# Layer 0 of a four-layer graph network: one pair's term sums shared between ScalarE and VectorE, with a third PSUM double bank and more closely spaced row loads

## The chip, the cores and the metric

The kernel runs on one core of one Trainium2 chip. The metric is the device time of one execution in microseconds (us), as a median over runs. The engines are called PE (TensorE), DVE (VectorE), ACT (ScalarE), POOL (GpSimd) and SP (SyncE); PE accumulates into PSUM, 8 banks of 128 x 512 float32, and everything else lies in SBUF. SP and POOL issue most DMA transfers here.

## The reference

`x` has shape (8, 2048, 64): 8 batches, N = 2048 nodes, 64 channels. `adj` is a row-normalised 2048 x 2048 matrix. Four layers follow each other, each as `x = layernorm(x + layer(x))`:

```
layer 0:  x0 = x, x1 = A x, x2 = 2 A (A x) - x                    (K = 3 diffusion steps)
          w[n,k] = sum_d emb[n,d] * weight[d,k]   (d = 0..15),  b = emb @ bias
          out[n] = sum_k xk[n] @ w[n,k] + b[n]
layer 1:  e = leaky_relu(s1[i] + s2[j]), masked by adj > 0.5, softmax over j, att @ x, elu
layer 2:  (A + I) (x W^T + b) / degree
layer 3:  three steps of  v = relu([v, A v] W1^T + b1) W2^T + b2
```

In layer 0 the weight matrix differs from node to node, but only through the 16 numbers `emb[n, :]`. So the kernel multiplies every node's stacked vector by all 16 base matrices, which gives 16 results ("terms") of 64 channels each, and then sums the terms with the factors `emb[n, d]`.

## The kernel before

All work is float32 except the masks (bfloat16). The 8 batches form four pairs (`NPAIR = 4`); a pair's values `SX[p]` are 128 columns wide and 16 tiles of 128 nodes long. A product with the adjacency matrix is a "sweep" (`sweep`, line 1040): for each of four column chunks, a PSUM bank from `acc_ring` collects 16 matmuls of 128 x 512 (line 1059), whose moving operand comes in "a-tiles" of 512 KB that SP loads (`fetch`, line 223) into 7 buffers. The sweeps run in a fixed order: A x for pairs 0 and 1 together, then A(A x) for each pair with A x of pairs 2 and 3 mixed in, then for each pair one sweep of layer 2 and three of layer 3.

What runs between the matmuls of the sweeps is not written out by hand. Every piece of work is a generator that yields an engine and what it waits for; `Plan.go` (line 82) repeatedly picks the one that can begin first by the plan's own costs, with a rank as tie-break, and so writes one fixed instruction order for each engine. `Ring` (line 96) hands out buffers and remembers when each was planned to be free. At run time each engine follows its order and waits on semaphores, so a planned cost that is off shows as a wait.

`rows_of_adj` (line 400) loads the 16 row tiles of `adj` (1 MB each, on SP, into `bc_ring`, 4 buffers) at the due times in its `yield`. `row_tile` (line 411) sums each row on ACT (line 414) and makes the mask on DVE (lines 417 to 420), which POOL stores to DRAM (line 423). The row maxima of layer 1 (line 706) load these masks again.

`second_pass` (line 553) is the last part of layer 0. For each tile of 128 nodes it has two halves `h` of eight terms. A half is four 512-wide products (line 578) into a double bank `yp` from `pp_ring`, which has two of them. `add_terms` (line 590) then reads `yp`. If a "terms" buffer was free in `e_ring` (4 buffers, shared with layer 1's `e`), ACT scales each term by its factor into that buffer (line 599), for both halves, and DVE adds the 16 terms as a tree of widths 1024, 512 and 256 (line 612) and two adds into `SX[p]` (line 614). If none was free, DVE does all 16 terms by multiply-and-add straight from PSUM (line 601). `first_norm` (line 621) adds the bias (line 625) and normalises a chunk of four tiles.

When a pair's four chunks are normalised, `layer1` (line 635) transposes the values (line 647), computes the score vectors (line 657), turns them into rows (`to_rows`, line 754; matmul at 759) and broadcasts these by DMA (line 682). DVE then finds row maxima (line 706, 32 per pair), and `weights` (line 773) makes each attention tile on DVE (784, 797) and ACT (792, 800), which PE applies to the values (`po`, line 810). `po_ring` has one double bank. `finish` (line 828) ends a half of layer 1, from the matmuls `pf` (line 845) on. `layer2_tail` (line 943) multiplies by W (`ps_emb`, line 947) and adds on DVE (line 956); `start_chunk` (line 967) normalises (last step at line 487), transposes (`ps_vT`, line 981), and `u_chunk` (line 990) prepares the operand of the next sweep (`ps_u`, line 994), copied by `copy` (line 337).

PSUM's eight banks are: `acc` 2 single banks, `pp` 2 double banks, `po` 1 double bank.

Of the kernel before, what the change touches and what calls it, by code (L numbers as in the profile page):

```python
# [17 lines left out]
P = 128  # L18
# [3 lines left out]
CW = N // NCH  # L22
# [113 lines left out]
def resnorm_d4_kernel(  # L136
# [22 lines left out]
    plan = Plan()  # L159
    at = plan.at  # L160
# [15 lines left out]
    pp_ring = Ring(ps, "pp", 2)  # L176
    po_ring = Ring(ps, "po", 1)
    bc_ring = Ring(wp, "bc", 4)
# [18 lines left out]
    def batches(v):  # L197

        if len(v.shape) == 3:
            v = v.rearrange("p t n -> p (t n)")  # L200
        return v.rearrange("p (b c) -> p b c", c=C)
# [198 lines left out]
    def rows_of_adj():  # L400


        for t in range(NT):
            yield "SP", [115.0 + 13.0 * t, bc_ring]
            an, k = bc_ring.take([P, 2, HALF], "an")
            an = an.rearrange("p a b -> p (a b)")
            nc.sync.dma_start(an, adj[t * P : (t + 1) * P, :])
            done = plan.run("SP", 2.8, bc_ring.t, 115.0 + 13.0 * t) + 9.0
            plan.start(1, row_tile(t, an, k, done))

    def row_tile(t, an, k, done):
        yield "ACT", [done]
        dg = tiny([P, 1], "dg", 2)
        nc.scalar.activation(an, an, AF.Copy, accum_out=dg)
        done = plan.run("ACT", act(N) + 0.2, done)
        yield "DVE", [done, mr_ring]
        nc.vector.tensor_scalar_add(dg, dg, 1.0)
        nc.vector.reciprocal(rdeg[:, t : t + 1], dg)
        mk, km = mr_ring.take([P, N], "mr", BF16)
        nc.vector.tensor_scalar(mk, an, THRESHOLD, NEG_INF, ALU.is_le, ALU.mult)  # L420
        done = plan.run("DVE", 1.13 + 0.16, done)
        bc_ring.give(k, done)
        nc.gpsimd.dma_start(by_row[t], mk)
        done = plan.run("DMA", 0.6, done) + 4.0
        mr_ring.give(km, done)
        at["by_row", t] = done + 2.0
        if all(("by_row", i) in at for i in range(NT)):
            at["rows"] = done
# [124 lines left out]
    def second_pass():  # L553

        for n in range(NPAIR * NCH):
            yield "PE", [("y2", n + 1), ("xg", n + 1)]
            p, c, y2T, ky, got = queue[n]
            xg, kx = stacked[n]
            left = [TPC]
            for j in range(TPC):  # L560
                t = c * TPC + j
                cs = slice(j * P, (j + 1) * P)
                for h in range(2):
                    hs = slice(h * CW, (h + 1) * CW)
                    if h == 0 or pp_ring.ready() > plan.free["PE"]:
                        yield "PE", [("xg", n + 1), got, pp_ring]
                    if h == 0:


                        terms = None  # L570
                        if e_ring.ready() < NEVER:
                            terms = e_ring.take([P, D0, P], "terms")
                    yp, k = pp_ring.take([P, 2, CW], "yp")

                    for k2 in (h, 1 - h):
                        for e in range(2):
                            rows = slice(e * C, (e + 1) * C) if k2 else slice(0, P)
                            nc.tensor.matmul(  # L578
                                yp[:, e, :],
                                lhsT=y2T[rows, cs] if k2 else xg[:, e, cs],  # L580
                                rhs=(wk2 if k2 else w01)[rows, hs],
                                start=(k2 == h),
                                stop=(k2 != h),
                            )
                    t_pe = plan.run("PE", 2.8, got)
                    plan.start((2, 2, 1, 1)[p], add_terms(p, c, t, h, yp, k, terms, t_pe, left))
            yt_ring.give(ky, t_pe)
            xg_ring.give(kx, t_pe)

    def add_terms(p, c, t, h, yp, k, terms, t_pe, left):  # L590
        eng = "ACT" if terms else "DVE"
        yield eng, [t_pe]
        v = SX[p][:, t, :]
        for d in range(8):
            dd = h * 8 + d
            term = yp[:, :, d * C : (d + 1) * C]
            weight = emb_sb[:, t, dd : dd + 1]
            if terms:
                nc.scalar.activation(batches(terms[0][:, dd, :]), term, AF.Copy, scale=weight)  # L599
            else:  # L600
                nc.vector.scalar_tensor_tensor(
                    batches(v), term, weight, batches(v), ALU.mult, ALU.add
                )
        done = plan.run(eng, 8 * (0.25 if eng == "ACT" else 0.265), t_pe)
        pp_ring.give(k, done)
        if h == 0:
            return
        if terms:
            yield "DVE", [done]
            for half in (8, 4, 2):  # L610
                a, b = (terms[0][:, i * half : (i + 1) * half, :] for i in range(2))
                nc.vector.tensor_tensor(a, a, b, ALU.add)  # L612
            for d in range(2):
                nc.vector.tensor_tensor(v, v, terms[0][:, d, :], ALU.add)
            done = plan.run("DVE", 2.5, done)
            e_ring.give(terms[1], done)
        left[0] -= 1
        if left[0] == 0:
            plan.start(2, first_norm(p, c, plan.free["DVE"] + plan.LAG))

    def first_norm(p, c, done):
        yield "DVE", [done]
        v = SX[p][:, tiles(c), :]
        v4 = v.rearrange("p t (e c) -> p t e c", c=C)
        nc.vector.tensor_tensor(
            v4, v4, eb[:, tiles(c), :].unsqueeze(2).to_broadcast([P, TPC, 2, C]), ALU.add
        )
        done = plan.run("DVE", dve(CW), done)
        done = yield from layer_norm(v, CW, done)
        at["n0", p, c] = done  # L630
        if all(("n0", p, i) in at for i in range(NCH)):
            at["x1", p] = max(at["n0", p, i] for i in range(NCH))
# [494 lines left out]
    ctx.enter_context(tc.manual_schedule())  # L1127
    plan.start(0, constants())
    plan.start(1, rows_of_adj())
    plan.start(1, stacks())  # L1130
    plan.start(2, second_pass())
    plan.start(3, tails())
    for p in range(NPAIR):
# [41 lines left out]
```

## Time and profile before

| what | value |
|---|---|
| median of 3 runs | 2182.61 us (2180.09 to 2184.45) |
| profiled execution | 2179.89 us, of which the span from first to last instruction 2178.1 us |
| DVE, tree of adds (L612), 58 of each width | 1024 wide 1222 ns, 512 wide 692 ns, 256 wide 425 ns |
| ACT, terms (L599), 928 instructions | 251.8 us busy |
| DVE, multiply-and-add from PSUM (L601), 96 instructions | 33.7 us busy, mean 351 ns |
| DVE, row maxima (L706), 128 instructions | 292.8 us busy, mean 2287 ns; first at 377.5 us |
| SP, loads of adjacency rows (L407), 16 of 1 MB | issued from 116.4 to 316.5 us, median 8.7 us from issue to landing |

The profile page gives the busy time and share of each engine, and then the span in 40 equal slices, one digit each in tenths of busy time. A line of the waits view says which instruction group waited for which, for how many us in total, how often, and the longest one. A line of the timeline gives start, duration, engine, source line, the tiles written and read, and in brackets the idle time before it with what ended it. One PE matmul of 128 x 512 in float32 appears as two records; consecutive records overlap, so a mean duration of one (about 0.6 us) is longer than the distance from one to the next (0.43 us). The line numbers are those of the kernel before; in the kernel after, lines 590 to 611 lie up to 6 lower in the file and all later ones 7 lower.

### The profile page before, as it was taken

The numbers are of one execution on the slowest core, as the hardware profiler recorded it, in microseconds if no ns is written. First come the engines' busy times: TensorE is split into PE (matmuls) and PEld (weight loads), VectorE is DVE, ScalarE is ACT, GpSimd is POOL, SyncE is SP. The second block draws the span as 40 slices with busy tenths as digits, with TensorE's granted clock in tenths as the row PEclk, the third lists the DMA queues.
The fourth block names the chain that finished last, engine by engine and source line by source line (L and its number), as shares of the span: only waits on it lengthen the run. The fifth ranks groups of instructions, "written<-read, shape, count | busy, mean of one in ns | idle before, by whom it ended". The sixth has DMA issues, their size and how long they took to land. (4 is left out here: it accounts for less than half of the span.)

```text
span 2178.1 us, 19094 instructions
## 1 busy us (share of the span) xinstructions
PE 2116.7 (97%) x6421; PEld 934.0 (43%) x6421; DVE 1424.8 (65%) x1823; ACT 973.0 (45%) x1761; POOL 194.6 (9%) x342
## 2 busy tenths in 40 slices
PE   8999999999999999999999999999999999999997
PEld 3444444433443333335443444444444544444443
DVE  2215554999789999989998989989797400121002
ACT  0016664467776555675724757417476200111001
POOL 2210000110011010000001011011010000000000
PEclk9999999999999999999999999999999999999999
DMA  9798764564344473347689778788787777887785
GB/s 312 270 323 297 241 201 146 165 208 123 113 159 122 132 245 110 121 129 258 214 304 345 237 274 297 255 307 292 241 270 226 247 263 269 282 289 247 265 277 182
DMA packets 228453, 504.26 MB, mean 232 GB/s; under 512 B 20530, under 2 KB 28850, under 8 KB 224242
## 3 DMA queue, kind: packets, MB, share of 16 engines
q1 hardware_dynamic: 189378, 372.79, 51.0%
q0 software_dynamic: 34752, 128.14, 17.4%
q10 hardware_dynamic: 4224, 2.10, 0.4%
q8 instruction: 51, 0.84, 0.2%
q14 instruction: 48, 0.39, 0.1%
HBM read 471.31 MB, written 29.56 MB: 230 GB/s over the span
## 5 line engine op out<-in xcount | busy, mean ns | idle before, releaser
L1059 PE MATMUL acc<-a,SX 128*128 128x512 f32 x1536 | 693.8, 597 | 9.4 <-DMA SX<-in_x 6.4
L1059 PE MATMUL acc<-a,SA 128*128 128x512 f32 x1280 | 575.0, 596 | 8.9 <-ACT SA L337 4.8
L1059 PEld LDWEIGHTS acc<-a,SX 128*128 128x128 f32 x1536 | 285.6, 191 | 350.7 <-issue 336.4
L1059 PEld LDWEIGHTS acc<-a,SA 128*128 128x128 f32 x1280 | 238.8, 191 | 293.9 <-issue 278.6
L792 ACT ACTIVATE e<-e,sv 128x1024 f32<-128x1024 f32 x256 | 280.9, 1153 | 108.8 <-DVE e L784 107.3
L706 DVE CUSTOM_DVE_ANT_0 junk<-s2b,mr 128x2048 bf16<-128x2048 f32 x128 | 292.8, 2287 | 24.3 <-DMA mr<-by_row 22.9
L800 ACT ACTIVATE e<-e 128x2048 f32<-128x2048 f32 x128 | 245.0, 1918 | 128.5 <-DVE e L797 128.0
L599 ACT ACTIVATE terms<-yp,emb_sb 128x128 f32<-128x128 f32 x928 | 251.8, 396 | 104.9 <-PE yp L578 104.8
L797 DVE TENSOR_TENSOR e<-e,mb 128x2048 f32<-128x2048 f32 x128 | 290.5, 2286 | 4.9 <-ACT e L792 4.7
L784 DVE TENSOR_TENSOR e<-s1b,mk 128x2048 f32<-128x2048 f32 x128 | 289.8, 2285 | 3.1 <-DMA mk<-by_col 3.1
L578 PE MATMUL yp<-SH,xgT 128*128 128x512 f32 x512 | 249.9, 611 | 5.3 <-issue 2.1
L810 PE MATMUL po<-e,SX 128*64 128x512 f32 x1024 | 236.4, 603 | 4.0 <-ACT e L800 4.0
L612 DVE TENSOR_TENSOR terms<-terms 128x1024 f32<-128x1024 f32 x174 | 135.7, 780 | 106.0 <-ACT terms L599 101.9
L578 PEld LDWEIGHTS yp<-SH,xgT 128*128 128x128 f32 x512 | 90.6, 190 | 149.9 <-issue 136.3
L578 PE MATMUL yp<-SH,y2T 64*128 64x512 f32 x512 | 131.3, 623 | 7.2 <-ACT terms L599 3.2
L810 PEld LDWEIGHTS po<-e,SX 128*64 128x64 f32 x1024 | 67.9, 137 | 160.1 <-issue 139.7
L1059 PE MATMUL acc<-a,SB 128*128 128x512 f32 x256 | 119.0, 594 | 0.0
L779 POOL DMA_DIRECT2D mk<-by_col x128 | 69.1, 541 | 537.7 <-DVE e L784 454.5
L919 ACT ACTIVATE SH<-acc,b31n 128x512 f32<-128x512 f32 x32 | 21.8, 681 | 209.8 <-PE acc L1059 209.8
L1003 DVE TENSOR_TENSOR SA<-ps_u,ceb 128x512 f32<-128x512 f32 x16 | 11.0, 689 | 118.5 <-PE ps_u L994 118.5
L1003 DVE TENSOR_TENSOR SX<-ps_u,ceb 128x512 f32<-128x512 f32 x16 | 11.0, 689 | 118.1 <-PE ps_u L994 118.1
L578 PEld LDWEIGHTS yp<-SH,y2T 64*128 64x128 f32 x512 | 42.9, 186 | 90.1 <-issue 78.7
(167 smaller groups left out, 1225.1 us busy)
## 6 DMA issues: line engine op xcount, KB each, us to landing
a<-in_adj_t SPq DMA_DIRECT2D x640, 512.0 KB, 5.2
mr<-by_row POOLq DMA_DIRECT2D x64, 512.0 KB, 5.7
mk<-by_col POOLq DMA_DIRECT2D x128, 256.0 KB, 5.2
an<-in_adj SPq DMA_DIRECT2D x16, 1024.0 KB, 8.7
a<-a_plus_i SPq DMA_DIRECT2D x32, 512.0 KB, 4.7
by_col<-mk POOLq DMA_DIRECT2D x32, 256.0 KB, 6.1
by_row<-mr POOLq DMA_DIRECT2D x16, 512.0 KB, 6.3
s2b<-s_rows POOLq DMA_DIRECT2D x8, 1024.0 KB, 7.3
```

The costliest lines, as they stand in the source:

```text
L578: nc.tensor.matmul(yp[:, e, :], lhsT=y2T[rows, cs] if k2 else xg[:, e, cs], rhs=(wk2 if k2 else w01)[rows, hs], start=(k2 == h), stop=(k2 ...
L599: nc.scalar.activation(batches(terms[0][:, dd, :]), term, AF.Copy, scale=weight)
L612: nc.vector.tensor_tensor(a, a, b, ALU.add)
L706: nc.vector.tensor_tensor_reduce(out=junk, in0=s2b[e][0], in1=masks[t][0], scale=1.0, scalar=LOWEST, op0=ALU.add, op1=ALU.max, accum_out=m ...
L779: nc.gpsimd.dma_start(mk, by_col[jt // 2][:, jt % 2, h * HALF : (h + 1) * HALF])
L784: nc.vector.tensor_tensor(e, s1b[0], mk.unsqueeze(1).to_broadcast([P, 2, HALF]), ALU.add)
L792: nc.scalar.activation(e[:, i, :], e[:, i, :], AF.Prelu, bias=sv[:, 2 + i, jt : jt + 1], alpha=ALPHA)
L797: nc.vector.tensor_tensor(e, e, mb[0], ALU.add)
L800: nc.scalar.activation(e, e, AF.Exp)
L810: nc.tensor.matmul(po[i * C : (i + 1) * C, f, :], lhsT=SX[p][:, t, i * C : (i + 1) * C], rhs=e[:, i, f * CW : (f + 1) * CW], start=(t == 0 ...
L1003: nc.vector.tensor_tensor(dst[:, tiles(c), :], pu, bias.unsqueeze(1).to_broadcast([P, TPC, P]), ALU.add)
L1059: nc.tensor.matmul(pa, lhsT=source[:, m, :], rhs=t[:, i, :], start=(m == 0 and not seed), stop=(m == NT - 1),)
```

## The change

Three edits belong together.

1. `rows_of_adj` spaces the due times of its loads by 9 instead of 13.
2. In `second_pass`, pair 0 takes its double bank from `po_ring` when that one is planned to be free earlier than those of `pp_ring`. So pair 0 has three double banks.
3. In `add_terms`, a tile of pair 0 that has a "terms" buffer is shared: ACT scales the eight terms of the first half, DVE multiplies and adds the eight of the second half straight into `SX[0]` (the form that was used before only without a buffer). DVE then adds only ACT's eight terms, a tree of widths 512 and 256 and the two adds. These adds now wait both for DVE's own half and for ACT's.

The planner orders all later work from these costs, so the order of instructions changes beyond pair 0 too.

```diff
         for t in range(NT):
-            yield "SP", [115.0 + 13.0 * t, bc_ring]
+            yield "SP", [115.0 + 9.0 * t, bc_ring]
...
-            done = plan.run("SP", 2.8, bc_ring.t, 115.0 + 13.0 * t) + 9.0
+            done = plan.run("SP", 2.8, bc_ring.t, 115.0 + 9.0 * t) + 9.0
...
                     hs = slice(h * CW, (h + 1) * CW)
-                    if h == 0 or pp_ring.ready() > plan.free["PE"]:
-                        yield "PE", [("xg", n + 1), got, pp_ring]
+
+                    ring = pp_ring
+                    if p == 0 and po_ring.ready() < pp_ring.ready():
+                        ring = po_ring
+                    if h == 0 or ring.ready() > plan.free["PE"]:
+                        yield "PE", [("xg", n + 1), got, ring]
...
-                    yp, k = pp_ring.take([P, 2, CW], "yp")
+                    yp, k = ring.take([P, 2, CW], "yp")
...
-    def add_terms(p, c, t, h, yp, k, terms, t_pe, left):
-        eng = "ACT" if terms else "DVE"
+    def add_terms(p, c, t, h, yp, ring, k, terms, t_pe, left):
+
+        shared = p == 0 and terms is not None
+        eng = "ACT" if terms and not (shared and h) else "DVE"
         yield eng, [t_pe]
...
-            if terms:
+            if eng == "ACT":
                 nc.scalar.activation(batches(terms[0][:, dd, :]), term, AF.Copy, scale=weight)
             else:
                 nc.vector.scalar_tensor_tensor(
                     batches(v), term, weight, batches(v), ALU.mult, ALU.add
                 )
         done = plan.run(eng, 8 * (0.25 if eng == "ACT" else 0.265), t_pe)
-        pp_ring.give(k, done)
+        ring.give(k, done)
         if h == 0:
+            at["terms", p, t] = done
             return
         if terms:
-            yield "DVE", [done]
-            for half in (8, 4, 2):
+            yield "DVE", [done, ("terms", p, t)]
+            for half in (4, 2) if shared else (8, 4, 2):
                 a, b = (terms[0][:, i * half : (i + 1) * half, :] for i in range(2))
                 nc.vector.tensor_tensor(a, a, b, ALU.add)
             for d in range(2):
                 nc.vector.tensor_tensor(v, v, terms[0][:, d, :], ALU.add)
-            done = plan.run("DVE", 2.5, done)
+            done = plan.run("DVE", 1.4 if shared else 2.5, done, ("terms", p, t))
             e_ring.give(terms[1], done)
```

More of the change, by code (lines that the diff above doesn't have):

```diff
@@ L585, in second_pass @@
                     t_pe = plan.run("PE", 2.8, got)
-                    plan.start((2, 2, 1, 1)[p], add_terms(p, c, t, h, yp, k, terms, t_pe, left))
+                    plan.start((2, 2, 1, 1)[p], add_terms(p, c, t, h, yp, ring, k, terms, t_pe, left))
             yt_ring.give(ky, t_pe)
             xg_ring.give(kx, t_pe)
-    def add_terms(p, c, t, h, yp, k, terms, t_pe, left):
-        eng = "ACT" if terms else "DVE"
+    def add_terms(p, c, t, h, yp, ring, k, terms, t_pe, left):
+        shared = p == 0 and terms is not None
+        eng = "ACT" if terms and not (shared and h) else "DVE"
         yield eng, [t_pe]
```

## Prediction, made before the changed kernel ran

> **What bounds the kernel now.** I read the page's busy table and slices first, then busy time by stage, then PE's waits, then the pieces of the timeline around the longest waits. "PE" is TensorE, "DVE" VectorE, "ACT" ScalarE.
>
> ```profile
> span 2178.1 us, 19094 instructions
> ...
> PE 2116.7 (97%) x6421; PEld 934.0 (43%) x6421; DVE 1424.8 (65%) x1823; ACT 973.0 (45%) x1761; POOL 194.6 (9%) x342
> ...
> PE   8999999999999999999999999999999999999997
> ...
> DVE  2215554999789999989998989989797400121002
> ```
>
> PE is busy nearly everywhere: only idle PE time can be saved, 2178.1 - 2116.7 = 61.4 us. DVE is at its limit from its eighth digit (381 us) to about the thirty-first, and half idle before. The next view is busy time in stretches: window, length, then PE, PEld, DVE, ACT, POOL.
>
> ```profile
> 146.00:310.00 164.00, 163.72 (x472) 69.82 (x472) 78.01 (x159) 99.19 (x294) 8.34 (x15) 1.00 0.77 263
> 310.00:361.00 51.00, 50.32 (x145) 21.53 (x144) 23.68 (x48) 27.84 (x90) 3.40 (x6) 1.00 0.40 129
> 361.00:440.00 79.00, 78.78 (x218) 33.47 (x218) 70.86 (x93) 33.67 (x114) 9.50 (x18) 1.00 0.59 194
> 440.00:1000.00 560.00, 540.39 (x1660) 214.49 (x1657) 519.82 (x639) 370.87 (x759) 56.44 (x103) 0.99 0.47 150
> 1000.00:1100.00 100.00, 94.84 (x350) 43.22 (x349) 98.00 (x109) 68.89 (x72) 9.76 (x19) 0.98 0.67 223
> 1100.00:1430.00 330.00, 320.01 (x1063) 146.91 (x1062) 303.07 (x324) 164.76 (x178) 37.63 (x68) 0.99 0.82 281
> ```
>
> The first row is the stage that the change edits: PE loses 0.28 us in it. So nothing is saved there directly. The loss sits where DVE is full: 19.6 us at 440-1000, 5.2 at 1000-1100, 10.0 at 1100-1430. Who PE waits for (total, times, longest):
>
> ```profile
> PE ps_vT L981 <- DVE SX L487: 5.2, 1, 5.2
> PE acc L1059 <- ACT SA L337: 4.8, 3, 3.5
> PE yp L578 <- ACT terms L599: 4.6, 5, 1.5
> PE po L810 <- ACT e L800: 4.0, 4, 2.1
> PE yp L578 <- DVE SX L601: 3.8, 3, 2.2
> ```
>
> Small waits behind vector work, almost none in pair 0's layer 0. An idle PE also costs more than the gap. Timeline of PE (start, duration, line, [idle before]):
>
> ```profile
> 468.50 7.07 PE L810 MATMUL po<-e,SX 128*64 128x512 f32 x24 [2.13 <-ACT e L800]
> ...
> 1030.68 5.37 PE L810 MATMUL po<-e,SX 128*64 128x512 f32 x24
> ...
> 1062.67 0.63 PE L981 MATMUL ps_vT<-ident,SB 128*128 128x128 f32 x4 [0.45 <-DVE SB L487]
> ...
> 1067.59 1.16 PE L994 MATMUL ps_u<-w31e,SH 128*128 128x128 f32 x8 [0.70 <-DVE SH L337]
> 1072.20 5.40 PE L1059 MATMUL acc<-a,SA 128*128 128x512 f32 x8 [3.46 <-ACT SA L337]
> ```
>
> The same 24 matmuls take 7.07 us after a 2.13 us gap and 5.37 without: 1.7 us more. The granted clock shows about five such places between 440 and 1430, some 8 us.
>
> **What the Trainium skill says.** "TensorE: Matmul & The Clock Gate", Part 1 (the HAM clock gate): after an idle window of about 3.4 us the array runs at half rate until about 3.4 us of work have passed. The trace shows the loss (1.7 us), but already after 2.13 us of idleness. "ScalarE: Activation LUTs", What ACT_TABLE_LOAD costs: an ACTIVATE with a per-partition operand takes about 280 ns + 0.833 ns per element, of which 93 ns overlap back to back: 387 and 294 ns for 128 elements. L599 has a median of 388 ns and, in a run of eight, 251.8 / 928 = 271 ns each. "PSUM — Partial Sum Buffer", Specifications: ScalarE and VectorE read PSUM in parallel at full rate unless they meet in one bank. The two halves lie in different double banks; no row of before isolates this.
>
> **The change part by part.** The durations are those of the profiled execution, 2179.9 us (span 2178.1), 2.7 us under the median of 2182.6. Counts come from the built programs' instruction orders.
>
> *Work on PE.* Both programs hold the same 3,345 matmul instructions; groups of po go from 64 to 62, runs of the y2T matmuls from 70 to 71. A split costs 0.15 to 0.2 us (x8 take 1.87 us, x16 3.58). Sum within 0.5 us: zero.
>
> *Halves shared.* Pair 0 has 16 tiles. On each, 8 ACT activations leave and 8 scalar_tensor_tensor (L601, 351 ns) come to DVE, while the 1024-wide add (L612, 1222 ns) goes: +2.81 - 1.22 = +1.59 us of DVE, 25.4 us in all. Pairs 1 to 3 also change: tiles without a "terms" buffer, all on DVE, go from 6 to 8. Each has 16 x 0.351 = 5.6 us instead of 1.22 + 0.69 + 0.43 + 0.58 = 2.9 of adds: +5.4 us. With some copies moved to ACT, DVE gets +30 us, ACT loses 160 x 0.271 = 43 us. In 146-310, where DVE is 78 of 164 us busy, this is hidden. The new waits there: a tile's adds on DVE wait for ACT's first half, and behind them in DVE's queue stand the row masks (L417 to L420) and the next tile's L601, for which PE's bank waits. ACT has its half 2.8 us of PE work before DVE gets the other and needs 2.2: cost 0, at most a few tenths per tile if ACT is late (16 x 0.3 = 5 us).
>
> *Third double bank.* The po bank stands idle until layer 1's first po matmul (466 us), so pair 0 may use it. PE's saving in place is at most that row's 0.28 us; its use is that six halves follow each other without sweep matmuls between them.
>
> *Denser rows.* The 16 loads of 1 MB stay, up to four in a row on SP's queue instead of two. The a-tiles queue behind them: 4 MB at 302 GB/s (the rate at 165-220) is 13.9 us, against seven a-tiles ahead, which feed at least 7 x 1.72 = 12 us of sweep and far more where yp stands between. A row load also waits for a buffer that DVE's L420 frees four rows earlier, and SP holds the a-tiles behind it. Cost 0 to 2 us (before has one such wait, 1.53 us at 144); I take 0. POOL issues the mask stores earlier, a few of them ahead of an xgT load instead of behind it, 0.54 us each, and 8 us busy of 164: 0. ACT's row sums (L414, 2.2 us) now stand three in a row ahead of one tile's terms, with the PE order leaving some 8 us there: 0.
>
> *What moves.* Adding measured durations in PE's order, the transpose of pair 0's score rows (L759), which starts layer 1, stands after 316.8 us of PE work instead of 351.4: a head start of 34.6 us. On the chip it ran at 360.8 and the first row maximum (L706) at 377.5, 16.7 us later (DMA and broadcast); I expect 326 and 343. The masks aren't late: the last row load stands nine a-tiles earlier in SP's order, some 45 us before its 316.5.
>
> *What the full DVE makes of it.* From the first L706 to the fourth L956 of pair 0 (layer 2's start) DVE has 633.4 us of work before and 671.1 after: +37.7. PE wants that fourth chunk after 1015.1 us of work before, 1021.6 after: +6.5. So DVE's room changes by 34.6 - 37.7 + 6.5 = **+3.4 us**. From there to the same point of pair 1: DVE 329.8 to 320.7, PE 337.7 to 329.7: +1.1. If PE's idle time in these stretches follows DVE's lateness, 4.5 us come back. Between the fourth ps_emb and its ps_vT, PE's order now holds 14.1 us of work instead of 11.5, so the waits of 0.45 and 0.70 us at 1062 and 1067 go, and perhaps 2 of the 3.46 after them: -3. The ACT copy of SA stays late behind the exponentials. Two more all-DVE tiles: waits on L601 were 3.8 + 0.9 us over 6 tiles, so 2 x 0.8 = +1.6. Sum: -4.5 - 3 + 1.6 = **-5.9 us**, 2174.0 for the profiled execution, **2176.7** for the median.
>
> The unknown in it is that waits sit at single places: a gap that crosses about 2 us costs 1.7 more. Four or five such places may appear or vanish: -8 to +8 around the sum.
>
> **The rivals.** *No change.* DVE's room is about the same (its share of PE's work is 95.4% before and 95.2% after in the first stretch), so PE loses the same microseconds elsewhere. For it: PE has no idle time in the edited stage, and what DVE is spared by starting early it pays back in added work. Against it: every pf (L845, the end of a half of layer 1) stands 6 to 53 us earlier in PE's work. Gives 2178.3 to 2187.
>
> *Slower: the head start is too small for the added DVE work.* Place: the first L706. With 37.7 us more work and 6.5 more time, DVE breaks even at a head start of 31.2 us; below it, PE waits one for one. It would shrink if pair 0's last chunk came late: PE's order puts the x transpose (L647) 16 us after the last yp, 29 before, and the chain between (8 STT 2.8, adds 1.7, bias and norm about 6.5) takes 11 to 12. A head start of 22 us costs 9: 2191 or so. For it: DVE is 95% full, and the margin is 3.4 us. Against it: the chain still fits by 3 to 4 us.
>
> *Clearly faster.* The earlier pf's take the waits at 1414 us (5.2, and 3.3 of clock loss) and the DMA waits away too: -15, 2168. Against it: pair 1's last ps_vT stands only 10 us behind its ps_emb, and DVE's queue has 11 us in between.
>
> *It doesn't do what it says:* the third bank is taken only where its ready time is earlier. PE's order shows three tiles in unbroken series, so it is used.
>
> **How the numbers follow.** A measurement here tells about 0.2%, 4.4 us, from no change. Faster as worked out or clearly so: 0.48. No change: 0.26. Slower: 0.26. The likeliest has 2176.7, its own range 2166 to 2182; the range that holds 8 in 10 runs from 2162 (clearly faster, with the bound on the waits) to 2191 (head start of 22 us).
>
> **What would show it.** Right: the first L706 near 343 us, L601 x256 at about 351 ns, L599 x768, PE's idle time at 146-310 still under 2 us, less idle time at 1000-1100, all PE work within a few us of 2116.7. Wrong: L706 after 347 us, waits on L601 above 8 us, PE waiting for a-tiles at 150-180, or gaps above 2 us with slow matmuls behind them where before has none.

## The result and the profile after

The changed kernel takes **2201.73 us** (2197.91 to 2204.61) against 2182.61 us: the ratio is **1.0083** with a 95% interval of 1.0062 to 1.0104, slower by 19 us. The forecast was 2176.7 us, range 2162 to 2191. The rest of this document asks why the sum was 25 us off.

The page of the profiled execution of the kernel after, in the rows shown of before:

```profile
span 2202.0 us, 19070 instructions
...
PE 2125.7 (97%) x6421; PEld 938.7 (43%) x6421; DVE 1452.6 (66%) x1957; ACT 931.5 (42%) x1601; POOL 195.5 (9%) x342
...
PE   8999999999999999999998999989999999999997
...
DVE  2227756999799999879998888989796200121002
```

The span grew by 23.9 us. PE's idle time went from 61.4 to 76.3 us (+14.9), and PE's busy time grew by 9.0 us although it holds the same matmuls: that is slow clock behind gaps (the last section has the clock's record). DVE has 27.8 us more work, ACT 41.5 less, nearly the +30 and -43 that were forecast. So the work was sized well, and the time was lost in waiting. Busy time in the same stretches as before (window, length, then PE, PEld, DVE, ACT, POOL), after:

```profile
146.00:310.00 164.00, 158.63 (x461) 67.68 (x460) 110.98 (x290) 73.25 (x184) 11.26 (x19) 0.99 0.77 272
310.00:361.00 51.00, 51.00 (x145) 22.07 (x145) 19.91 (x33) 19.20 (x67) 3.81 (x7) 1.00 0.52 170
361.00:440.00 79.00, 76.53 (x203) 32.49 (x202) 77.63 (x94) 34.92 (x108) 13.24 (x24) 0.98 0.65 211
440.00:1000.00 560.00, 541.76 (x1687) 216.55 (x1686) 515.98 (x645) 369.20 (x732) 52.06 (x94) 0.99 0.45 140
1000.00:1100.00 100.00, 95.05 (x341) 42.40 (x341) 96.24 (x121) 61.68 (x80) 9.15 (x17) 1.00 0.66 222
1100.00:1430.00 330.00, 313.94 (x1027) 143.28 (x1024) 293.48 (x310) 161.60 (x171) 36.42 (x66) 0.99 0.81 278
```

Subtract PE's busy time from each length. In the edited stage, PE's idle time is 5.37 us instead of 0.28; at 361-440 it is 2.47 instead of 0.22; at 440-1100 it is 23.2 instead of 24.8, a small gain; at 1100-1430 it is 16.1 instead of 10.0. PE's waits (total, times, longest) name new places:

```profile
PE yp L582 <- ACT terms L605: 9.7, 6, 4.9
...
PE acc L1066 <- ACT SA L337: 5.1, 5, 2.1
PE ps_u L1001 <- ACT SH L926: 4.6, 1, 4.6
...
PE po L817 <- ACT e L807: 3.7, 3, 2.2
```

The wait of 5.2 us on ps_vT is gone, as hoped. A wait of 4.9 on the terms and one of 4.6 on ps_u have come. A gap's cost also includes the slow matmuls after it, so I counted differently: for each amount of PE work, taken in PE's order with usual durations, when was it done? This is how far a kernel lies behind the kernel before (us), worked out from the traces. A column that lies right on a loss can be off by a few us, since it depends on what is taken as usual:

```
PE work done (us)            100   200   300   450   900  1050  1300  1400   end
after                        1.4   7.8   7.1  14.5   9.6   6.2  15.1  27.3  24.0
e3 before's order, more DVE  1.2   0.9   3.9   4.9   5.2   6.7   6.7   6.4   6.4
e4 after's order, old work   1.0   8.6   7.1  13.2   9.4   8.0  13.4  21.9  18.7
e5 after, 3 mask buffers     0.7   0.5   4.3   9.5   6.9   4.4   8.0  16.4  13.2
e1 rows at 9                 0.5  -0.1   4.8   5.8  11.0   9.8  16.9  26.4  23.6
e13 rows at 11               0.5   0.0   0.3   6.6   3.0   6.3  17.6  28.9  26.1
e14 rows at 12               0.9   3.0   2.6   4.0   9.7   8.2  13.0  21.5  19.4
e17 rows at 14              -0.1  -0.1   0.6   1.9   2.8   1.3   2.3  11.3   8.4
e8 after, measured costs     1.0   1.1   0.5  -0.4 -22.9 -22.7 -20.7 -28.2 -25.7
```

After loses 6.4 us around 200, 7 around 450 (given back by 1050), and 21 between 1050 and 1400, on the way to and at the start of layer 2 of pair 1. The first loss in the timeline of after (start, duration, engine, line, [idle before]):

```profile
186.16 1.23 DVE L420 TENSOR_SCALAR mr<-an 128x2048 bf16<-128x2048 f32 x1 [8.68 <-DMA by_row<-mr]
187.30 3.05 DVE L607 SCALAR_TENSOR_TENSOR SX<-yp,emb_sb,SX 128x128 f32<-128x128 f32 x8
...
195.20 0.63 ACT L469 ACTIVATE ln_sq<-SX 128x512 f32<-128x512 f32 x1 [10.88 <-DVE SX L462]
195.73 1.89 ACT L414 ACTIVATE an<-an 128x2048 f32<-128x2048 f32 x1
...
197.97 1.89 ACT L414 ACTIVATE an<-an 128x2048 f32<-128x2048 f32 x1
...
199.86 4.22 ACT L605 ACTIVATE terms<-yp,emb_sb 128x128 f32<-128x128 f32 x16
...
202.06 2.08 PE L582 MATMUL yp<-SH,y2T 64*128 64x512 f32 x4 [4.89 <-ACT terms L605]
```

DVE waits 8.68 us for the store of an earlier mask to free one of two buffers. Behind it in DVE's queue stand a half's L607 and a normalisation; ACT waits 10.88 us for that normalisation, and then two row sums (L414) stand ahead of the terms, which begin another 4.0 us later; PE waits 4.89 us for the bank. One wait crosses three in-order queues.

The 21 us after 1050 of PE work come at three places: some 7 at 1171 us, 5 at 1352 (`ps_emb` after a gap of 3.10 us) and 8 or more at 1417 to 1448. The one at 1171 has the same form as the first loss:

```profile
1162.01 2.29 DVE L713 CUSTOM_DVE_ANT_0 junk<-s2b,mr 128x2048 bf16<-128x2048 f32 x1 [7.90 <-DMA mr<-by_row]
...
1166.55 4.39 ACT L799 ACTIVATE e<-e,sv 128x1024 f32<-128x1024 f32 x4 [22.63 <-DVE e L791]
1170.84 0.67 ACT L926 ACTIVATE SH<-acc,b31n 128x512 f32<-128x512 f32 x1
1171.57 2.08 PE L1001 MATMUL ps_u<-ge,SH 128*128 128x128 f32 x8 [4.55 <-ACT SH L926]
```

DVE waits for a mask, ACT for DVE's attention tiles, and the activation that PE needs stands on ACT behind the exponentials of these tiles. The third place, the start of pair 1's layer 2, PE alone:

```profile
1418.16 3.60 PE L1066 MATMUL acc<-a,SA 128*128 128x512 f32 x8
1423.10 1.16 PE L852 MATMUL pf<-back,poT 128*128 128x130 f32 x8 [1.34 <-ACT SH L337]
1426.59 1.34 PE L1001 MATMUL ps_u<-w31e,SH 128*128 128x128 f32 x8 [2.33 <-DVE SX L963]
1428.61 6.48 PE L1066 MATMUL acc<-a,SA 128*128 128x512 f32 x8 [0.68 <-ACT SA L337]
1436.53 0.63 PE L988 MATMUL ps_vT<-ident,SX 128*128 128x128 f32 x4 [1.44 <-DVE SX L487]
1439.11 2.08 PE L1001 MATMUL ps_u<-w31e,SH 128*128 128x128 f32 x8 [1.94 <-ACT SH L337]
```

Each step of the chain (normalise, transpose, multiply, copy) finds PE early by 0.7 to 2.3 us, and eight records of 512-wide matmuls take 6.48 us; the same eight take 3.60 us at full clock ten us before (first line).

### The profile page after: what moved, and what is told of

Its sections match the earlier page's. It is cut to its first block, busy times and chain, and to the rows that moved or that the text cites. A ratio compares the mean times of both kernels' runs of the same rounds, so it can differ in the third digit from the quotient of the medians.

```text
span 2202.0 us, 19070 instructions
## 1 busy us (share of the span) xinstructions
PE 2125.7 (97%) x6421; PEld 938.7 (43%) x6421; DVE 1452.6 (66%) x1957; ACT 931.5 (42%) x1601; POOL 195.5 (9%) x342
## 5 line engine op out<-in xcount | busy, mean ns | idle before, releaser
L713 DVE CUSTOM_DVE_ANT_0 junk<-s2b,mr 128x2048 bf16<-128x2048 f32 x128 | 292.7, 2287 | 32.9 <-DMA mr<-by_row 31.7
L582 PE MATMUL yp<-SH,xgT 128*128 128x512 f32 x512 | 250.7, 615 | 1.5 <-ACT terms L605 0.7
L605 ACT ACTIVATE terms<-yp,emb_sb 128x128 f32<-128x128 f32 x768 | 207.9, 396 | 68.5 <-PE yp L582 68.4
L582 PEld LDWEIGHTS yp<-SH,xgT 128*128 128x128 f32 x512 | 92.4, 193 | 146.8 <-issue 138.3
L582 PE MATMUL yp<-SH,y2T 64*128 64x512 f32 x512 | 134.5, 633 | 16.1 <-ACT terms L605 8.9
L619 DVE TENSOR_TENSOR terms<-terms 128x512 f32<-128x512 f32 (+1 forms) x152 | 111.1, 731 | 35.6 <-ACT terms L605 32.2
L607 DVE SCALAR_TENSOR_TENSOR SX<-yp,emb_sb,SX 128x128 f32<-128x128 f32 x256 | 89.7, 350 | 48.4 <-PE yp L582 39.8
L469 ACT ACTIVATE ln_sq<-SX 128x512 f32<-128x512 f32 x48 | 30.4, 633 | 165.0 <-DVE SX L462 77.8
```

The costliest lines, as they stand in the source:

```text
L582: nc.tensor.matmul(yp[:, e, :], lhsT=y2T[rows, cs] if k2 else xg[:, e, cs], rhs=(wk2 if k2 else w01)[rows, hs], start=(k2 == h), stop=(k2 ...
L607: nc.vector.scalar_tensor_tensor(batches(v), term, weight, batches(v), ALU.mult, ALU.add)
L713: nc.vector.tensor_tensor_reduce(out=junk, in0=s2b[e][0], in1=masks[t][0], scale=1.0, scalar=LOWEST, op0=ALU.add, op1=ALU.max, accum_out=m ...
```

## The experiments

Every time is a median beside runs of the kernel before on the same chip, with the ratio's 95% interval. Theories: **B**, the added DVE work; **C**, the mask buffer at 202 us, with **M**, mask buffers in general; the new instruction **order** (**A**; from e5 on **L**, a lottery of orders) and, behind it (**P**, then **P1**), a plan whose costs are too short. The expectations on record say what each gives.

**The change taken apart (e1, e2).** Kernel before with only `13.0 * t` → `9.0 * t` in both places of `rows_of_adj`; and the kernel after with the rows back at 13:

> The kernel before with the first edit alone: adjacency-row loads due every 9 instead of 13. Theory A (each new instruction order meets the chip with its own set of waits, and the order of the kernel after happens to have more): the order changes here too, so the time moves by some us in either direction, -8 to +15 us, although no work is added. Theory B (the 25 us of vector work that pair 0 gets on DVE, which is full from 340 us on, is what costs): this kernel adds none, so within 4 us of before. Theory C (the dense loads slow the mask stores, DVE waits for a mask buffer and PE behind it): +4 to +7 us, all of it between 150 and 215 us.

> The kernel after with the row loads back at 13: halves shared and third bank alone. Theory C: the wait of 4.9 us at 202 and DVE's wait of 8.7 us for a mask buffer are gone, so 5 to 7 us less than after, about +12 us over before. Theory B: the vector work is all there, so +12 to +19 us over before, with the losses after 400 us unchanged. Theory A: another order, so anything from -5 to +20 us over before, and the losses after 400 us stand at other places than in after.

Denser rows alone: 2203.73 us, 1.0094 [1.0073, 1.0116]. Sharing and third bank alone: 2189.47 us, 1.0028 [1.0020, 1.0037]. The rows alone lose as much as the whole change, though they add only 6.8 us of work to DVE (1431.6 us busy) and take 8.0 from ACT. The two parts (+20.8, +6.5) don't add up to the whole (+19). The +20.8 lies beyond all three ranges on record, nearest to A's; the +6.5 fits A alone.

**Work against order (e3, e4).** The instructions are changed without the plan knowing, so PE's, SP's and POOL's orders stay exactly those of the parent. e3 is before with after's work for pair 0:

```diff
-            if terms:
+            if terms and not (p == 0 and h):      # line 598: the second half on DVE
...
-            for half in (8, 4, 2):
+            for half in (4, 2) if p == 0 else (8, 4, 2):
```

e4 is the reverse on after: `if eng == "ACT"` becomes `if terms`, and the tree has its 1024-wide add again.

> The kernel before with pair 0's second halves computed on DVE, while the planner still books them on ACT: PE, SP and POOL have the very order of before, DVE 25 us more work, ACT 35 us less. Theory A (the new order is the loss): within 4 us of before, because pair 0's stage hides the work. Theory B (the added DVE work is the loss): +10 to +20 us. Theory C: within 2 us.

> The kernel after with pair 0's second halves computed on ACT again, while the planner still books them on DVE: PE, SP and POOL have the very order of after, DVE 25 us less work, ACT 35 us more. Theory A: as slow as after downstream, +12 to +25 us over before. Theory B: the loss is gone or halved, 0 to +8 us over before. Theory C: the loss before 215 us stays (4 to 8 us).

The work in before's order: 2186.28 us, 1.0014 [1.0007, 1.0021], +3.4 us. After's order with the old work: 2196.11 us, 1.0061 [1.0042, 1.0079], +13.2 us. So the order alone carries most of the loss, and the added DVE work 3 to 6 us (2201.7 - 2196.1 = 5.6). B is too small; e4's row of the table stays within 1.8 us of after's as far as 1300, losing at the same places.

**Mask buffers (e5, e6, e7).** A third real buffer for the masks, with unchanged plan and orders (`real=3` makes the tiles rotate over three tags while the plan still counts two). To make room, `ln_sq`, `ex` and `eb` are held in bf16.

```diff
-    mr_ring = Ring(wp, "mr", 2)
+    mr_ring = Ring(wp, "mr", 2, real=3)
```

> The kernel after with every engine's instruction order unchanged, but three buffers for the row masks (mr) where the planner books two; for room, the squares in the layer norm, elu's exponentials and the embedding bias are kept in bfloat16. Theory M (the new orders lose because DVE, in order, stands in front of row masks that come late through two buffers, and normalisations and attention tiles behind it make PE wait): DVE's waits on DMA for mr (31.7 us) and for the mask store (8.7 us) mostly go, and with them the PE waits at 202, 1171 and 1352 to 1442 us: 10 to 16 us faster than after, that is +3 to +9 us over before. Theory L (the orders are a lottery of planned against real times on all engines, the masks are only one of many): 0 to 5 us faster than after, +14 to +19 over before.

> The kernel before, same order on every engine, with three buffers for the row masks (and the same three tensors in bfloat16 as in e5_after_mr3). Its DVE waits 22.9 us for masks. Theory M: part of its PE waits go too, among them that of 5.2 us at 1414: -3 to -8 us. Theory L: within 4 us of before.

> The kernel of e1_rows9 (row loads at 9, nothing else), same order on every engine, with three buffers for the row masks (and the three tensors in bfloat16). DVE waits 24.2 us for masks there, and PE 10.3 us at 1439. Theory M: 8 to 15 us faster than e1_rows9, +6 to +13 us over before. Theory L: 0 to 5 us faster, +16 to +21 us over before.

On after 2192.41 us, 1.0038 [1.0023, 1.0053], some 10 us back; on before 2181.35, 0.9991 [0.9984, 0.9998]; on e1 2203.52, 1.0089 [1.0074, 1.0104], nothing. So M fits in after, just, and L in the other two, where mask buffers and bfloat16 together give 2.3 us or less; bfloat16 alone was not run. What DVE waits for among the masks, after and e5 (L715 is L713 there):

```profile
DVE junk L713 <- DMA mr<-by_row: 31.7, 12, 7.9
...
DVE mr L420 <- DMA by_row<-mr: 8.7, 1, 8.7
```

```profile
DVE junk L715 <- DMA mr<-by_row: 22.7, 7, 7.1
```

The wait at 186 us is gone in e5, and the table shows 0.5 instead of 7.8 at 200. But e5 has lost 5.6 us by 250: its next yp waits 2.68 us for ACT's terms at 217 (L416 is L414 there, L607 L605, L584 L582):

```profile
213.39 1.91 ACT L416 ACTIVATE an<-an 128x2048 f32<-128x2048 f32 x1 [8.79 <-DMA an<-in_adj]
...
215.30 2.16 ACT L607 ACTIVATE terms<-yp,emb_sb 128x128 f32<-128x128 f32 x8
...
217.51 3.68 PE L584 MATMUL yp<-SH,xgT 128*128 128x512 f32 x4 [2.68 <-ACT terms L607]
```

The terms stand on ACT behind a row sum, and that waits 8.79 us for its adjacency row. e1 has the same at 260 us: ACT waits 5.76 us for a row, PE then 2.14. Such waits add up to 6.6 us in before, 13.2 in after, 14.3 in e1 and 20.1 in e5, so the denser rows do cost a few us here. Most of the rest that e5 gains lies at 1171, where its PE no longer waits for `ps_u`. So C is a true cause in after, but not of the loss in general, and part of what it frees is lost at the next late place: e1 loses as much in the end with a wait for a mask buffer of no more than 0.6 us, and M gives it nothing back.

**The plan's costs (e8 to e12).** What the profile measures was put in place of what the plan assumes: a multiply-and-add 0.351 (DVE) and an activation 0.271 us (ACT), a shared tile's adds 1.7, a full tree 2.95, a row maximum 2.33. Nothing else in the kernel changes: nearly the same work, newly ordered.

```diff
-        done = plan.run(eng, 8 * (0.25 if eng == "ACT" else 0.265), t_pe)
+        done = plan.run(eng, 8 * (0.271 if eng == "ACT" else 0.351), t_pe)
...
-            done = plan.run("DVE", 1.4 if shared else 2.5, done, ("terms", p, t))
+            done = plan.run("DVE", 1.7 if shared else 2.95, done, ("terms", p, t))
...
-                    done = plan.run("DVE", 2.25, ("mask", p, t), ready)
+                    done = plan.run("DVE", 2.33, ("mask", p, t), ready)
```

> The kernel after, but the planner books what the profile measured: 0.351 us instead of 0.265 for a multiply-and-add on DVE, 0.271 instead of 0.25 for a term on ACT, 1.7 instead of 1.4 and 2.95 instead of 2.5 us for the adds, 2.33 instead of 2.25 for a row maximum. Theory P (the loss is that the plan books DVE too short, by some 14 us over the whole kernel, so PE's order is too optimistic): 8 to 18 us faster than after, 0 to +10 us over before. Theory L: another order, anywhere from +2 to +22 us over before. Theory M: the masks are still late, so +10 us or more.

> The kernel before with the measured costs of e8_after_costs in its planner and nothing else. Theory P1 (planning with true durations is worth some 28 us to either kernel, and the change is worth little by itself): 2150 to 2165 us. Theory P2 (the true durations matter only for the kernel after, whose pair 0 puts far more multiply-and-adds on DVE; before was planned well enough): within 6 us of before, so that the change with a true plan is a gain of over 20 us.

> The kernel of e1_rows9 (row loads at 9 alone, 20.8 us over before) with the measured costs in its planner. It has no shared halves. Theory P1: the 20.8 us are gone and it stands within 6 us of e9_before_costs. If the dense loads themselves cost (mask stores and row loads in each other's way), it stays 10 to 20 us over e9_before_costs.

> The kernel of e2_share_rows13 (shared halves and third bank, rows at 13) with the measured costs in its planner. Under P1 within 6 us of e9_before_costs and of e8_after_costs; under P2 it tells whether the gain of e8_after_costs needs the dense rows: 2154 us if not, over 2165 if it does.

> The kernel after with one cost alone put right, the multiply-and-add on DVE (0.351 instead of 0.265 us). If this one, which is off by 22 us over 256 instructions, is what misleads the plan: 2150 to 2170 us. If the smaller errors (terms on ACT, the adds, the row maxima, together some 50 us too short over the kernel) matter as much: 2175 to 2200 us.

After: **2154.08 us**, 0.9864 [0.9849, 0.9879]. Before: 2158.66, 0.9892 [0.9877, 0.9907]. Rows at 9: 2153.84, 0.9867 [0.9851, 0.9883]. Sharing with rows at 13: 2166.52, 0.9926 [0.9909, 0.9943]. After with the multiply-and-add alone corrected: 2181.54, 1.0000 [0.9991, 1.0008], 20 of the 47.6 us. Every version with all the costs gains 23 to 50 us over its own parent. For e8 that is far past every range on record (P had 8 to 18 us); e12 fell where the smaller errors matter as much. Page and PE's waits of e8:

```profile
span 2152.5 us, 19050 instructions
...
PE 2110.3 (98%) x6421; PEld 934.3 (43%) x6421; DVE 1456.7 (68%) x1977; ACT 924.4 (43%) x1571; POOL 194.8 (9%) x342
```

```profile
PE ps_vT L988 <- DVE SB L487: 4.3, 1, 4.3
PE yp L582 <- ACT terms L605: 4.0, 5, 1.3
...
PE acc L1066 <- ACT SA L337: 2.0, 3, 0.7
```

DVE does 4 us more than in after, but PE idles 42.2 us instead of 76.3 and its busy time falls by 15.4 us as the clock stays up. The stretch in which pair 1 starts layer 2, in before, after and e8 (PE, PEld, DVE, ACT, POOL, then PE's clock):

```profile
1320.00:1450.00 130.00, 124.11 (x410) 58.42 (x409) 122.84 (x150) 59.52 (x69) 15.18 (x28) 0.97 0.81 275
```

```profile
1320.00:1450.00 130.00, 117.43 (x373) 54.00 (x372) 118.96 (x147) 58.38 (x70) 11.58 (x22) 0.92 0.74 254
```

```profile
1320.00:1450.00 130.00, 128.65 (x430) 60.08 (x429) 124.62 (x139) 57.57 (x66) 16.68 (x31) 1.00 0.84 293
```

PE idles 5.9, 12.6 and 1.4 us there, at a clock of 0.97, 0.92 and 1.00. DVE is as full as before. It is not faster in e8; PE has more other work until DVE is ready. Last `ps_emb` of the pair and its `ps_vT`, in before and e8:

```profile
1401.46 1.05 PE L947 MATMUL ps_emb<-w2bd,z 128*128 128x128 f32 x8
...
1414.59 1.08 PE L981 MATMUL ps_vT<-ident,SX 128*128 128x128 f32 x4 [5.21 <-DVE SX L487]
```

```profile
1374.48 1.16 PE L954 MATMUL ps_emb<-w2bd,z 128*128 128x128 f32 x8
...
1388.74 0.60 PE L988 MATMUL ps_vT<-ident,SX 128*128 128x128 f32 x4
```

In before PE has 7 us of other work between the two and then waits 5.21; in e8 it has 13 us and no gap. P1 holds for the size; it had also said that all versions would come within 6 us, and they span 12.7: with rows at 13, sharing still costs 7.9 us (2166.52 - 2158.66). Whether the costs must be true, or only longer, is not shown: no plan with costs above the measured ones was run.

**Density or a redrawn order (e13 to e18).** The spacing alone was changed to 11, 12 and 14, on before, on after (11) and with measured costs (11).

> The kernel before, with the due times of the adjacency rows spaced by 11 instead of 13 and nothing else. If density itself costs time (each microsecond of spacing taken away delays something in proportion), this lies about halfway to the 20.8 us that spacing 9 lost: +8 to +12 us over the kernel before. If spacing only redraws the instruction order, and each order has its own sum of waits at single places, it can land anywhere: -8 to +20 us, and on no line with 13, 12 and 9.

> The kernel before with spacing 12. Density: +3 to +7 us over the kernel before, below spacing 11. Redrawn order: anywhere from -8 to +20 us; a value above that of spacing 11, or below the kernel before, rules out density alone.

> The whole change, but with rows spaced by 11. Density: between the 6.5 us lost at 13 and the 19 us lost at 9, so +10 to +15 us. Redrawn order: outside that as likely as inside, -4 to +25 us.

> The whole change with rows spaced by 11 and the planner's four costs as measured. If true costs take the waits away whatever the order, it stands between the 2154.1 us (spacing 9) and 2166.5 us (spacing 13) of the same costs, about 2160. If the order is still redrawn by a few us with true costs, it may fall outside these two, 2150 to 2172; the scatter over the three spacings then says how much of the 4.6 us between the changed and the old kernel with true costs belongs to the change.

> The kernel before with spacing 14, looser than its own 13. Density: no slower than before, about 2180 to 2183 us. Redrawn order: the spacings 12, 11 and 9 gave 2201.3, 2202.4 and 2203.7 us, so 2182.9 us would be one good draw, and this lands near the others, 2190 to 2210 us.

> The kernel before with spacing 11 and the planner's costs as measured; the same with the sharing and the third bank took 2150.7 us. If those two edits are worth by themselves what the prediction gave them under a true plan, this is 2155 to 2159 us. If they are worth nothing (at spacing 9 the two differ by 0.3 us), 2149 to 2153 us.

All medians by spacing (us; a dash was not run):

```
spacing of the row loads       14        13        12        11         9
plan's costs, not shared   2191.2    2182.6    2201.3    2202.4    2203.7
plan's costs, shared            -    2189.5         -    2192.7    2201.7
measured, not shared            -    2158.7         -    2155.4    2153.8
measured, shared                -    2166.5         -    2150.7    2154.1
```

Ratios of the new ones, in order of the labels: 1.0083 [1.0066, 1.0100], 1.0082 [1.0066, 1.0098], 1.0044 [1.0029, 1.0059], 0.9848 [0.9833, 0.9862], 1.0039 [1.0025, 1.0053], 0.9871 [0.9854, 0.9888].

Spacing 12 loses nearly as much as 9, and 14 also loses. A cost that grows steadily with density gives neither. With measured costs the denser rows are faster (9 against 13: -4.8 and -12.4 us), so the load itself doesn't cost 20 us; the few us of late rows above are outweighed. The first table adds to this: e1, e13 and e14 end within 7 us of each other but lose by different routes (4.8, 0.3 and 2.6 us at 300; 11.0, 3.0 and 9.7 at 900), and all three, like e17, lose 8 to 11 us against before at 1300-1400, as after does (12). What was not settled is whether a weak tendency against density remains under the plan's own costs: leaving out 13, the values do rise from 14 to 9. The third bank was never run without the shared halves, so neither has a value of its own.

The eight orders under the plan's costs take 2183 to 2204 us; the seven other than before average 2197.5. Before's is the lowest, 15 us below that mean. The six under measured costs take 2151 to 2167. **The fastest is e16, 2150.65 us** (2148.36 to 2151.23): sharing, third bank, rows at 11, measured costs.

## Why the prediction was wrong, point by point

- **The durations and counts held.** L607 ran 256 times at 350 ns (forecast x256, 351), L605 768 times; DVE +27.8 us for +30, ACT -41.5 for -43. PE's waits on L607 for more tiles without a buffer, priced at +1.6 us, didn't come: 3.9 us instead of 4.7.
- **The head start nearly held.** The first row maximum ran at 350.5 us, for 343 forecast; about 6 us of that is PE's lateness, nearly all from the stall at 202. In PE work the first row maximum stands 33.5 us earlier, above the break-even of 31.2, so the slower rival was right in sign and wrong in its mechanism. Two signs of being wrong that the text named came true: L706 after 347 us, and gaps above 2 us with slow matmuls behind them.
- **"Cost 0" for the masks and row sums in pair 0's stage failed.** The text named the row masks as queued behind the adds, and the row sums "three in a row ahead of one tile's terms", but didn't follow what the masks themselves wait for: a buffer that a store frees, late (the stores landed in a median of 5.9 us, and this one took long enough to hold DVE 8.68). The row sums then did delay the terms, by 4.0 us at 196, and they also wait for their rows, which the text priced at zero too. Priced at zero with "the PE order leaving some 8 us there", this stage cost 6.4 us. e5, which takes the mask's wait away, is 7.3 us ahead of after at 200, but only 2.7 at 250, because a row sum is late there.
- **The first stretch came out near the sum.** From 250 to 1050 us of PE work after goes from 8.3 to 6.2 us behind: a gain of 2.1 where 4.8 (3.4 + 3 - 1.6) was forecast. In the pair-0 chain the waits of 0.45 and 0.70 us went and the 3.46 behind them did not: after has 1.53 and 2.12 us for the same copy of SA at 1061 and 1087.
- **The term that failed most is the +1.1 us of room for pair 1's start of layer 2.** From 1050 to the end after loses 17.8 us. The sum of DVE work against PE work was right and said little: room is an average over the stretch, and PE lost time at single places inside it, where the order puts a consumer a few us too early or behind a wait of another engine (1171, 1352 and 1417 to 1448 us). e4, with the old work in after's order, loses 10.7 us of it, and e3, with the new work in before's order, nothing. The text had this as an unknown of -8 to +8 around the sum. The e1, e13 and e14 orders, with about the work of before, cost +19 to +21, so its size was about 20, and it was not centred on zero.
- **Why not centred.** Before has the lowest time of the eight orders written with the plan's costs, so another order was likely to lose; why it is the lowest isn't shown. What the text could have seen is that such an order isn't kept on the chip: the code assumes 0.265 us for a multiply-and-add that its own profile showed at 0.351 (eight take 3.05 us in the timeline above, planned 2.12; even 0.351 books only 2.81). The text quotes the 0.351 and prices DVE with it, but took the order that a plan with 0.265 wrote as if PE could keep it. The short costs hold for before as well, so they explain the level of all eight orders and not by themselves the distance between before and after. With the four measured costs before no longer stands out: 2158.7 us among 2150.7 to 2166.5. Correcting the multiply-and-add alone goes with 20 us (e12) and the others with 27 more (e8), but 20 us is also the width of the draw of orders, so this split, of one order each, is not sure.
- **The change's own worth.** With the four measured costs in the plan, after against before is 2154.08 - 2158.66 = -4.6 us, close to the forecast -5.9. But the parts don't support the reasons: sharing and third bank at equal spacing give +7.9, -4.7 and +0.3 us at 13, 11 and 9, no gain that stands out from the scatter of orders, and at 9 the -4.8 goes with the denser rows, priced at zero. That agreement is luck.

## What to carry to other kernels

In a kernel whose instruction order comes from a planner, any edit redraws the order, and that can weigh more than the edit: compare the planner's costs with the profile's durations first, and mend them before judging anything else. A sum of work by stage bounds what can be won; the time is decided by single waits in in-order queues, so for each moved step follow what it waits for itself, down to the buffer and the DMA that frees it. A few harmless variations of one number (here a spacing) tell how wide the draw of orders is, and whether the starting point is a good draw; without that width, one comparison says little about an edit.

## What the runs showed of the hardware that was not expected

Short gaps on PE are followed by slow matmuls, but not at a fixed price. After has 14.9 us more idle time on PE than before and 9.0 us more busy time for the same matmuls; e13 has 20.4 and 6.3 more, e17 8.7 more idle time and 0.6 less busy time. The clock records of the traces show what lies between: ahead of the last 12 us the granted clock stands at one half for 44 us in after, 20 in before and 17 in e8, in pieces of 3.4 us or two or three times that. The prediction took a gap of about 2 us as the point from which 1.7 us are added. But of the eight gaps of 2.0 to 2.8 us in after, four are followed by half clock (at 426, 468, 747 and 1426 us) and four are not (650, 855, 1087 and 1159 us). In 19 of the 20 profiles one such piece begins at 78 to 81 us, where PE has had no gap above 0.1 us for ten us, but has just run 32 small matmuls (`ps_eb`) whose operands lie on 16 of the 128 partitions.

The section of the Trainium skill cited in the prediction ("TensorE: Matmul & The Clock Gate", Part 1) speaks of an idle window of about 3.4 us and, further on, of frequent short idle times that have the same effect, without a price for them. The half clock and the pieces of 3.4 us agree with it. But here the matmuls after gaps of only 1.3, 2.3 and 0.7 us in a row ran eight records in 6.48 us instead of 3.60, and the mean clock from 1320 to 1450 us was 0.92.
